# A cross-attention block: Fc's weight sums, some loads, and the last output projection placed and computed differently

## The chip, the cores and the metric

The kernel runs on one core of a Trainium2 chip. The metric is the device time of one execution in microseconds (us). Of three runs of the kernel before, the median is 766.39 us, the lowest 765.56 and the highest 767.55.

## The reference

One transformer block with cross-attention, in float32: batch 4, 512 positions, width 512, 16 heads of 32, MLP width 2048.

```python
residual = x
y = layer_norm(x, ln1_w, ln1_b)
q = (y @ q_w + q_b).reshape(B, LQ, H, HD).transpose(0, 2, 1, 3)
k = (enc @ k_w + k_b) ...        # enc: the other sequence, 512 positions too
v = (enc @ v_w + v_b) ...
scores = where(mask, q @ k^T / sqrt(HD), mask_value)
out = softmax(scores) @ v                      # back to B, LQ, D
hidden = out @ cproj_w + cproj_b + residual
y = layer_norm(hidden, ln2_w, ln2_b)
y = gelu_tanh(y @ fc_w + fc_b) @ proj_w + proj_b      # 512 -> 2048 -> 512
return hidden + y
```

## The kernel before

**Pairs.** The heads of a batch are taken in 4 groups of 4, so there are 16 windows w = 4 b + g, and each is done in two halves of 256 queries: 32 pairs p = 2 w + half (batch 0 is pairs 0 to 7, batch 3 pairs 24 to 31). `block` does one pair: TensorE writes 8 score tiles of 128x512 (`scores`, L317); VectorE adds the mask and takes the row minimum of the negated scores (L323); ScalarE takes the exponential with the row sums (L327); VectorE transposes the probabilities in squares of 32 into the tile tb (L335), of which there are two.

**The exchange.** The squares of tb have then to change places between groups of 32 partitions, into one tile of probabilities: pT, or for pairs 1, 3, 5, 7 the tile gt and for pairs 25, 27, 29, 31 the tile xe. `copies` does it: GpSimd copies the four squares that stay in their partitions (L393, 32x1088 each), and SyncE issues 12 DMAs for the others (L398). `attend` multiplies the result by v (L415, tile av), and VectorE scales it into oT (L420). There is one pT, so a pair's exchange is begun by `exchange` only when `attend` has read the pair before that in the same tile. From pair 10 on, `attend` of pair p - 2 runs at the start of pair p.

**The rest as filling.** The order on every engine is written out by hand: the program is recorded instruction by instruction and nothing reorders it. `put(p, ...)` lists what else is issued in pair p: projections of later windows (`prep_k` L255, `prep_q` L267, `prep_v`), layer norms, output projections, and, from pair 11 on by `some(n)`, the MLP of batches 0 and 1. Work of one item costs one product chain (3.4 in the planner's units, `CHAIN`) or two; `fill` deals it out between the steps of `block`.

**The MLP.** Fc works on pairs of 128-row chunks of fc_w by a form of Strassen's scheme: seven products of quarters in place of eight (`fc_seven`, products L576, sums on VectorE L530). Four sums of weight quarters are needed for each pair of chunks; GpSimd makes them ahead (`fc_sums`, four operations of 128x256 on wsum and pbt, L527 and L530), and for batch 0 stores them to DRAM by two DMAs of its own (L619, L620), as later batches read them again. `fc_sums` is called after every MLP item (in `fc_by_pair` and `proj`), directly behind `load_mlp`, and works on what has been loaded. wsum holds two sets. `proj` is the second MLP product (tile accp, L636).

**Layer norm of batches 1 and 3.** It is done on x transposed: `load_raw` loads the rows (tiles raw), the statistics come from a straight copy of x, `store_rn` and `load_rn` spread reciprocal deviation and mean over the partitions by way of DRAM (tiles rn), `ln1_rows` applies them on GpSimd (L218, 8 operations of 128x512) and `ln1_affine` weight and bias on ScalarE, into the tile xe, whose first half holds enc. Batches 0 and 2 use `load_x` and `ln1` (the items x1, x2, x3, and x4 = `load_enc`).

**Output projection.** `cproj(b, t)` multiplies 128 positions of oT by wc in four matmuls of 512 columns (L455, tile accc) and VectorE adds the result (L456) to h, which holds x and on which GpSimd has put the bias (`c_bias`, L426). Batch 3's h lies in the tile pbt.

**Queues.** Nearly all loads, the exchange, and batch 3's stores of h (tensor xa) are issued by SyncE, in one order; one of its DMAs is held until the eighth before it has landed. PSUM's eight banks are two pools of four, used in turns.

**The tail.** Behind pair 31 stand the last two `attend`, the MLP items left, `p_sums` (sums of proj's weight quarters, VectorE), batch 3's `cproj`, and `last_mlps`: the MLP of batches 2 and 3, whose weights for the next Fc pair are loaded by `load_wa`.

Of the kernel before, what the change touches and what calls it, by code (L numbers as in the profile page):

```python
# [12 lines left out]
F32 = mybir.dt.float32  # L13
# [38 lines left out]
def xattn_block(ctx: ExitStack, tc: tile.TileContext, x, rawT, encT, mask, q_w, k_w, v_w, c_w, fc_w, p_w, vecs, rows, out):  # L52
# [124 lines left out]
    def load_enc(b):  # L177
        for d in range(ND):
            queue(b).dma_start(out=eT[:, d, :], in_=encT[b, ts(d, P), :])
# [271 lines left out]
    def cproj(b, t):  # L451
# [5 lines left out]
        if not stays(b, t):  # L457
            (nc.sync if b == B - 1 else nc.gpsimd).dma_start(out=S["xa", b][ts(t, P), :], in_=h)

    def load_xn(b):  # L460

        for t in range(NT):
            S["h", b, t] = tiles.tile([P, D], F32, tag="xn", name=f"hn_{b}_{t}")
            Q[0].dma_start(out=S["h", b, t], in_=S["xa", b][ts(t, P), :])
# [144 lines left out]
    def fc_sums():  # L609

        while count[3] < len(fc_pairs) and count[3] < count[4] + 2:
            b, c = fc_pairs[count[3]]
            if ("fcw", b, 2 * c + 1) not in S:
                return
            x, y = raw_pair(b, c)
            s = wsum[:, count[3] % 2]
            a_sums(x[:, :2], x[:, 2:], y[:, :2], y[:, 2:], s[:, 0], s[:, 1], y[:, :2], s[:, 2], nc.gpsimd)
            if b == 0:
                nc.gpsimd.dma_start(out=sums_dram[c, :, :3], in_=s)  # L619
                nc.gpsimd.dma_start(out=sums_dram[c, :, 3], in_=y[:, :2])  # L620
            S["ws", b, c] = s[:, 0], s[:, 1], y[:, :2], s[:, 2]
            count[3] += 1

    def fc_by_pair(b, c):
        q, k = divmod(2 * c, FQ)
        fc_seven(b, c, gT[q % 2][:, k : k + 2, :], raw_pair(b, c), S["ws", b, c], acc_half, q % 2)
        count[1] += 2
        count[4] += 1
        load_mlp()
        fc_sums()  # L630

    def proj(b, q, t):
        gelus(q % 2)
        acc = acc_tile(f"accp_{b}_{q}_{t}")
        for k in range(FQ):
            nc.tensor.matmul(  # L636
                acc, gT[q % 2][:, k, ts(t, P)], S["pw", b, q * FQ + k], start=(k == 0), stop=(k == FQ - 1)
            )
        h = S["hid", b, t]
        nc.vector.tensor_tensor(h, acc, h, ALU.add)  # L640
        if q == NQ - 1:
            (nc.gpsimd if b == 0 else nc.sync).dma_start(out=out[b, ts(t, P), :], in_=h)
        count[1] += 1
        load_mlp()
        fc_sums()

# [22 lines left out]
    def last_mlps():  # L669
        last, = pools(ctx, last=1)  # L670
        ps_last = banks.pop()
        assert count[5] % 8 < 4
        count[5] = 0
        ga = last.tile([P, NP, 2, L], F32, tag="ga", name="ga")
        gs = last.tile([P, 3, NP, HL], F32, tag="gs", name="gs")
# [226 lines left out]
    def do(fn):  # L902
        return [(0.0, fn)]
# [62 lines left out]
    prep_v(0)  # L966
    prep_k(1)
    run(turns1(0))
    load_raw(1)
    load_h(0, *range(NT))  # L970
    nc.sync.dma_start(out=wc, in_=c_w)
    load_mlp()
# [24 lines left out]
    def h_(b, *ts_):  # L997
        return do(lambda: load_h(b, *ts_))
# [27 lines left out]
    k5, q5, v5 = A(5)  # L1026
    k6, q6, v6 = A(6)
    put(0, [(CHAIN, lambda: prep_v(1)), v2], do(lambda: store_rn(1)), [k2])
    put(1, [k3, (0.0, lambda: prep_q(1)), (CHAIN, lambda: (prep_v(3), load_enc(1), load_rn(1)))])
    put(2, [q2], [k4], do(lambda: ln1_rows(1, 0, 1)))  # L1030
    put(3, [q3, v4], do(lambda: ln1_rows(1, 2, 3)))
    put(4, [k5, v5], do(lambda: ln1_affine(1)))
    put(5, [q4, q5])
    put(6, [k6, q6])
# [10 lines left out]
    put(11, [k, v], some(2), pb_(0), mid=do(lambda: y_sums(0)))  # L1045

    x1, x2, x3, x4 = inputs(3)
    put(12, [q], some(2), x1)
    k, q, v = A(10)
    put(13, [k], some(2))  # L1050
    put(14, [q], some(2))
    put(15, x2[:1], V(10), x2[1:2], do(lambda: load_raw(3)), some(2), do(lambda: store_rn(3)), some(1),
        do(lambda: load_rn(3)), some(1))

    k, q, v = A(11)
    put(16, do(lambda: ln1_rows(3, *range(ND))), [k, q], some(2))
    put(17, h_(1, 0, 1), next_(lambda: ln1_affine(3)), h_(1, 2, 3), x4, cb(1), C(1))
    k, q, v = A(12)
    put(18, [q], some(2), [k])
    k, q, v = A(13)  # L1060
# [20 lines left out]
    for p in range(2 * NW):  # L1081
        w, half = divmod(p, 2)
        if half == 0 and w and w % NG == 0:
            make_mb(w // NG)
        run(ahead[p])
        for pair in due.get(p, ()):
            attend(*divmod(pair, 2))

        def fill(n, work=fills[p]):
            if n or not work or work[0][0] <= CHAIN:  # L1090
                run(work, CHAIN if n < 2 else None)

        block(w, half, fill, any(cost > CHAIN for cost, _ in fills[p]), mids[p])
# [3 lines left out]
    load_h(B - 1, *range(NT))  # L1097
    run(stat(2, 0, 1))
    attend(NW - 1, 0)
    run(some(2) + stat(2, 2, 3) + rs(2) + cb(B - 1) + norm(2, 0, 1) + some(2))  # L1100
    load_wa(first_c)
    attend(NW - 1, 1)
    run(mlp + norm(2, 2, 3))
    p_sums(first_c)
    load_wa(first_c + 1)
    c = C(B - 1)
    run(c[:2])
    p_sums(first_c + 2)
    run(c[2:])
    att.close()  # L1110
    last_mlps()

# [44 lines left out]
```

## Time and profile before

| | |
|---|---|
| median of three runs | 766.39 us (765.56 to 767.55) |
| profiled execution, its time | 765.46 us |
| its span, first to last instruction | 763.7 us |
| granted TensorE clock | 1.000 |
| busy: TensorE / VectorE / ScalarE / GpSimd | 757.0 / 591.2 / 336.5 / 329.3 us |
| chain that ended last | TensorE 93%, DMA 4%, SyncE's queue 2%, VectorE 1% |
| moved by DMA | 134.58 MB, mean 176 GB/s |

All times of the profile are of that one execution, on a clock that starts with its span; it took 0.93 us less than the median. PE is TensorE, DVE VectorE, ACT ScalarE, POOL GpSimd, SP SyncE, and SPq SyncE's queue of DMAs. In the timeline a row is a run of like instructions of one line, with its start, its length, and in brackets the idle time ahead of it with what ended it.

### The profile page before, as it was taken

The numbers are of one execution on the slowest core, as the hardware profiler recorded it, in microseconds if no ns is written. First come the engines' busy times: TensorE is split into PE (matmuls) and PEld (weight loads), VectorE is DVE, ScalarE is ACT, GpSimd is POOL, SyncE is SP. The second block draws the span as 40 slices with busy tenths as digits, with TensorE's granted clock in tenths as the row PEclk, the third lists the DMA queues.
The fourth block names the chain that finished last, engine by engine and source line by source line (L and its number), as shares of the span: only waits on it lengthen the run. The fifth ranks groups of instructions, "written<-read, shape, count | busy, mean of one in ns | idle before, by whom it ended". The sixth has DMA issues, their size and how long they took to land.

```text
span 763.7 us, 12836 instructions
## 1 busy us (share of the span) xinstructions
PE 757.0 (99%) x4346; PEld 512.8 (67%) x4346; DVE 591.2 (77%) x1186; ACT 336.5 (44%) x765; POOL 329.3 (43%) x347
## 2 busy tenths in 40 slices
PE   9999999999999999999999999999999999999998
PEld 7655455566574545475454566447888889988997
DVE  3888999879895777887887989855777886747862
ACT  2566766565773574637753567401202221022200
POOL 1538647368564874244575534430050014303152
PEclk9999999999999999999999999999999999999999
DMA  8999879467876686665756867783724402146001
GB/s 328 334 250 243 218 202 258 109 204 210 249 222 212 171 251 198 163 181 125 179 133 186 214 202 187 172 291 131 268 98 135 163 27 90 35 135 217 1 15 42
DMA packets 60576, 134.58 MB, mean 176 GB/s; under 512 B 11312, under 2 KB 17072, under 8 KB 60384
## 3 DMA queue, kind: packets, MB, share of 16 engines
q1 hardware_dynamic: 58448, 126.73, 57.3%
q0 software_dynamic: 1920, 7.01, 2.8%
q8 instruction: 35, 0.57, 0.3%
q14 instruction: 29, 0.24, 0.1%
q10 hardware_dynamic: 144, 0.02, 0.0%
HBM read 69.23 MB, written 11.02 MB: 105 GB/s over the span
## 4 chain that ended last, share of the span: by engine, by line
PE 93%; DMA 4%; SPq 2%; DVE 1%; issue 0%; POOL 0%; POOLq 0%
PE q L576 24%; PE accp L636 11%; PE r L723 8%; PE av L415 8%; PE accc L455 7%; PE sc L317 7%; PE acck L255 7%; PE accq L267 6%; PE accv L278 3%; PE accv L298 3%; PE q4p L759 2%; PE q1p L777 2%; SPq L398 2%; PE tp L166 1%; DMA pbt<-fc_w_dram 1%; DMA ptt<-v_w_dram 1%
## 5 line engine op out<-in xcount | busy, mean ns | idle before, releaser
L327 ACT ACTIVATE ptt<-ptt,mn 128x512 f32<-128x512 f32 x256 | 181.6, 711 | 143.0 <-DVE mn L323 142.9
L323 DVE CUSTOM_DVE_ANT_0 ptt<-sc,mb 128x512 f32<-128x512 f32 x256 | 160.6, 682 | 19.3 <-PE sc L317 19.2
L335 DVE STREAM_TRANSPOSE tb<-ptt 128x1024 f32<-128x1024 f32 x128 | 153.3, 1217 | 0.0
L393 POOL COPY pT<-tb 32x1088 f32<-32x1088 f32 x96 | 104.7, 1090 | 58.8 <-DMA pbt<-p_w_dram 19.0
L636 PE MATMUL accp<-pbt,gt 128*128 128x512 f32 x192 | 84.8, 595 | 0.0
L576 PE MATMUL q<-yT,gt 128*128 128x256 f32 x320 | 78.9, 379 | 0.0
L597 ACT ACTIVATE ga<-ga,vec 128x512 f32<-128x512 f32 x40 | 26.7, 714 | 92.3 <-DVE ga L530 92.3
L576 PEld LDWEIGHTS q<-yT,gt 128*128 128x128 f32 x320 | 60.8, 190 | 8.7 <-issue 0.2
L636 PEld LDWEIGHTS accp<-pbt,gt 128*128 128x128 f32 x192 | 35.9, 190 | 45.1 <-issue 39.9
L317 PE MATMUL sc<-pbt 32*128 32x512 f32 x512 | 65.3, 614 | 0.0
L576 PE MATMUL q<-ys,gt 128*128 128x256 f32 x240 | 61.6, 379 | 0.0
L255 PE MATMUL acck<-xe,ptt 128*128 128x512 f32 x128 | 58.5, 600 | 0.7 <-DVE tb L335 0.7
L267 PE MATMUL accq<-xe,ptt 128*128 128x512 f32 (+1 forms) x136 | 58.5, 574 | 0.0
L455 PE MATMUL accc<-wc,oT 128*128 128x512 f32 x128 | 56.5, 597 | 0.0
L530 DVE TENSOR_TENSOR ga<-q,ga 128x512 f32<-128x512 f32 (+1 forms) x60 | 36.2, 603 | 21.8 <-PE q L576 20.0
L576 PEld LDWEIGHTS q<-ys,gt 128*128 128x128 f32 x240 | 45.6, 190 | 6.2
L327 ACT ACTIVATION_READ_ACCUMULATOR ptt<-ptt,mn 128x1 f32 x256 | 47.8, 187 | 0.0
L415 PE MATMUL av<-pT,v 128*32 128x256 f32 x768 | 46.4, 382 | 1.4 <-DMA pT<-tb 0.7
L267 PEld LDWEIGHTS accq<-xe,ptt 128*128 128x128 f32 x136 | 24.9, 190 | 31.4 <-issue 22.5
L455 PEld LDWEIGHTS accc<-wc,oT 128*128 128x128 f32 x128 | 23.8, 190 | 31.6 <-issue 27.2
L255 PEld LDWEIGHTS acck<-xe,ptt 128*128 128x128 f32 x128 | 23.4, 191 | 31.6 <-issue 22.2
L317 PEld LDWEIGHTS sc<-pbt 32*128 32x128 f32 x512 | 27.3, 183 | 24.9 <-issue 15.8
(190 smaller groups left out, 1228.4 us busy)
## 6 DMA issues: line engine op xcount, KB each, us to landing
pT<-tb SPq DMA_DIRECT2D x288, 136.0 KB, 2.4
pbt<-p_w_dram SPq DMA_DIRECT2D x40, 256.0 KB, 3.8
gt<-ws SPq DMA_DIRECT2D x20, 512.0 KB, 3.4
gt<-tb SPq DMA_DIRECT2D x48, 136.0 KB, 4.3
xe<-tb SPq DMA_DIRECT2D x48, 136.0 KB, 2.8
pbt<-fc_w_dram SPq DMA_DIRECT2D x24, 256.0 KB, 3.5
gt<-fc_w_dram SPq DMA_DIRECT2D x20, 256.0 KB, 3.3
ptt<-k_w_dram SPq DMA_DIRECT2D x16, 256.0 KB, 3.3
```

Of the source, the lines that this page charges most:

```text
L255: nc.tensor.matmul(acc, S["wk", w][:, d, :], eT[:, d, :], start=(d == 0), stop=(d == ND - 1))
L267: nc.tensor.matmul(acc, S["wq", w][:, d, :], xT[:, d, c], start=(d == 0), stop=(d == ND - 1))
L317: nc.tensor.matmul(S["sc", w, qt][h], qT[r, ts(qt, P)], kT[r, :], start=True, stop=True)
L323: nc.vector.tensor_tensor_reduce(out=s, in0=S["sc", w, qt][h], in1=S["mb", w // NG], scale=1.0, scalar=FMAX, op0=ALU.add, op1=ALU.min, acc ...
L327: nc.scalar.activation(s, s, AF.Exp, bias=mn, scale=-1.0, accum_out=S["sums", w][:, qt, h : h + 1])
L335: nc.vector.transpose(tv[:, qt % 2, 2 * k : 2 * k + 2], S["ps", w, qt, k])
L393: nc.gpsimd.tensor_copy(pT[ts(i, HD), i], tb[ts(i, HD), i])
L415: nc.tensor.matmul(av[ts(h, HD), : 2 * P].rearrange(shape, **kw), v[:, t, ts(h, HD)], p[t][h], start=(t == 0), stop=(t == NT - 1),)
L455: nc.tensor.matmul(acc, S["oT", b][:, g, ts(t, P)], wc[:, g, :], start=(g == 0), stop=(g == NG - 1))
L576: nc.tensor.matmul(o, x[:, k], y[:, k], start=(k == 0), stop=(k == 1))
L636: nc.tensor.matmul(acc, gT[q % 2][:, k, ts(t, P)], S["pw", b, q * FQ + k], start=(k == 0), stop=(k == FQ - 1))
L723: nc.tensor.matmul(r, x[:, c], w[:, c], start=(c == 0), stop=(c == NP // 2 - 1))
```

## The change

1. Batch 3's output projection is no longer four `cproj` but `cproj_last`: the 512x512x512 product is cut into quarters and done by seven products of 256 (q1 to q7), each with four matmuls of 256 columns. The sums of wc's quarters go into the tile wct, those of oT's into oTt (both take the place of a tb); the results are joined with h on VectorE, three of the joins on GpSimd. The parts stand between the remaining MLP items, and the layer norm of positions 256 to 511 of batch 2 (`norm(2, 2, 3)`) goes behind them.
2. `fc_sums` is no longer called behind each MLP item but once a pair, after `attend`, for p > 10, and by that behind the exchange's copies.
3. Batch 1's raw rows (`load_raw(1)`) are loaded in pair 1 instead of at the start, its spread rows (`load_rn(1)`) in pair 2 instead of 1, and `ln1_rows` of batch 1 stands as a whole in pair 3.
4. x of batch 3 (x1) is loaded in pair 14 instead of 12; the first two tiles of h of batch 1 in pair 16 instead of 17.

```diff
+    def cproj_last():
+        b = B - 1
+        wt, ot = (two.tile([P, NI, PW + 2 * HD], F32, tag="tb", name=n) for n in ("wct", "oTt"))
...
+        a11, a21, a12, a22 = (S["oT", b][:, 2 * k : 2 * k + 2, ts(i, HL)] for k in range(2) for i in range(2))
+        w11, w12, w21, w22 = (wc[:, 2 * k : 2 * k + 2, ts(j, HL)] for k in range(2) for j in range(2))
+        t1, t2, t4, p1, u2, u3 = (wt[:, n] for n in range(6))
+        s1, s2, s4 = (ot[:, n] for n in range(3))
+        s3, t3 = a21, w12
...
+        def product(n, x, w):
+            q[n] = acc_half(f"q{n}c")
+            for t in range(2):
+                for k in range(2):
+                    nc.tensor.matmul(q[n][:, t], x[:, k, ts(t, P)], w[:, k], start=(k == 0), stop=(k == 1))
+        def join(engine, i, j, src):
+            o = h[:, 2 * i : 2 * i + 2, ts(j, HL)]
+            add(engine, o, src, o)
...
+        def one():
+            b_sums(w11, w12, w21, w22, t1, t2, t3, t4)
+            sub(s3, a11, a21)
+        def two_():
+            product(1, a11, w11)
+            nc.scalar.copy(p1, q[1])
+            product(2, a12, w21)
+        def three():
+            product(7, s3, t3)
+        def sums():
+            sub(s2, a22, s3)
+            sub(s4, a12, s2)
+            add(nc.vector, s1, s2, a11)
+        def four():
+            product(6, s2, t2)
+            add(nc.vector, u2, q[6], p1)
+            product(3, s4, w22)
+            add(nc.vector, u3, q[7], u2)
+            product(5, s1, t1)
+            join(nc.gpsimd, 1, 0, u3)
+            join(nc.gpsimd, 1, 1, u3)
+            join(nc.gpsimd, 0, 1, u2)
+            join(nc.vector, 0, 0, q[1])
+            join(nc.vector, 0, 0, q[2])
+        def five_():
+            product(4, a22, t4)
+            join(nc.vector, 0, 1, q[3])
+            join(nc.vector, 0, 1, q[5])
+            for t in range(2):
+                store(t)
+            join(nc.vector, 1, 1, q[5])
+            join(nc.vector, 1, 0, q[4])
+            for t in range(2, 4):
+                store(t)
...
     def fc_by_pair(b, c):     # and the same line in proj
         load_mlp()
-        fc_sums()
...
-    load_raw(1)
...
-    put(1, [k3, (0.0, lambda: prep_q(1)), (CHAIN, lambda: (prep_v(3), load_enc(1), load_rn(1)))])
-    put(2, [q2], [k4], do(lambda: ln1_rows(1, 0, 1)))
-    put(3, [q3, v4], do(lambda: ln1_rows(1, 2, 3)))
+    put(1, [k3, (0.0, lambda: prep_q(1)), (CHAIN, lambda: (prep_v(3), load_enc(1), load_raw(1)))])
+    put(2, [q2], [k4], next_(lambda: load_rn(1)))
+    put(3, [q3, v4], do(lambda: ln1_rows(1, *range(ND))))
...
-    put(12, [q], some(2), x1)
+    put(12, [q], some(2))
-    put(14, [q], some(2))
+    put(14, [q], some(2), x1)
...
-    put(16, do(lambda: ln1_rows(3, *range(ND))), [k, q], some(2))
-    put(17, h_(1, 0, 1), next_(lambda: ln1_affine(3)), h_(1, 2, 3), x4, cb(1), C(1))
+    put(16, do(lambda: ln1_rows(3, *range(ND))), [k, q], some(2), h_(1, 0, 1))
+    put(17, next_(lambda: ln1_affine(3)), h_(1, 2, 3), x4, cb(1), C(1))
...
             attend(*divmod(pair, 2))
+        if p > 10:
+            fc_sums()
...
     attend(NW - 1, 0)
-    run(some(2) + stat(2, 2, 3) + rs(2) + cb(B - 1) + norm(2, 0, 1) + some(2))
+    c = cproj_last()
+    c[0]()
+    run(some(2) + do(c[1]) + stat(2, 2, 3) + rs(2) + cb(B - 1) + norm(2, 0, 1) + some(1) + do(c[2]))
     load_wa(first_c)
     attend(NW - 1, 1)
-    run(mlp + norm(2, 2, 3))
+    c[3]()
+    run(mlp)
+    c[4]()
     p_sums(first_c)
     load_wa(first_c + 1)
-    c = C(B - 1)
-    run(c[:2])
+    c[5]()
+    run(norm(2, 2, 3))
     p_sums(first_c + 2)
-    run(c[2:])
```

**TensorE, the tail.** Before, from the av of pair 30 to the first Fc of batch 2 (accp are MLP projections of batch 1, accc the output projection of batch 3; L455, L636):

```order
L415 MATMUL av_0_4395<-pT_0_4246,v_3508 32x256 x16
L636 MATMUL accp_1_0_4413<-pbt,gt 128x512 x4
L636 MATMUL accp_1_1_4419<-pbt,gt 128x512 x4
L636 MATMUL accp_1_2_4441<-pbt,gt 128x512 x4
L636 MATMUL accp_1_3_4447<-pbt,gt 128x512 x4
L415 MATMUL av_1_4460<-xe,v_3508 32x256 x16
L455 MATMUL accc_0_4487<-wc,oT_3710 128x512 x4
L455 MATMUL accc_1_4494<-wc,oT_3710 128x512 x4
L455 MATMUL accc_2_4505<-wc,oT_3710 128x512 x4
L455 MATMUL accc_3_4512<-wc,oT_3710 128x512 x4
L576 MATMUL q_1_4_4533<-yT_3367,gt 128x256 x2
```

The same place of the change, where the seven products are q1c to q7c and Fc's line is now L646, that of the MLP projections L705:

```order
L705 MATMUL accp_1_1_4426<-pbt,gt 128x512 x4
L479 MATMUL q1c<-wc,oT_3710 128x256 x4
L479 MATMUL q2c<-wc,oT_3710 128x256 x4
L705 MATMUL accp_1_2_4459<-pbt,gt 128x512 x4
L479 MATMUL q7c<-wc,oT_3710 128x256 x4
L415 MATMUL av_1_4473<-xe,v_3508 32x256 x16
L705 MATMUL accp_1_3_4494<-pbt,gt 128x512 x4
L479 MATMUL q6c<-wct,oTt 128x256 x4
L479 MATMUL q3c<-wc,oTt 128x256 x4
L479 MATMUL q5c<-wct,oTt 128x256 x4
L479 MATMUL q4c<-wct,oT_3710 128x256 x4
L646 MATMUL q_1_4_4566<-yT_3367,gt 128x256 x2
```

Three products now stand ahead of the last av, one MLP projection behind it, and four products between that and Fc.

**SyncE, the start.** Before, from the last v weight to pair 1's exchange; the raw loads stand further up, behind the first weights:

```order
L248 DMA ptt<-v_w_dram 128x512
L179 DMA xe<-encT_dram 128x512 x4
L213 DMA rn_0_499<-rn_381 128x512
L213 DMA rn_1_500<-rn_381 128x512
L398 DMA gt<-tb_1_410 32x1088 x12
L248 DMA ptt<-q_w_dram 128x512
```

The same place of the change (rn and raw are the tiles of batch 1, rn_373 the DRAM tensor that is spread):

```order
L248 DMA ptt<-v_w_dram 128x512
L179 DMA xe<-encT_dram 128x512 x4
L200 DMA raw_0_491<-rawT_dram 128x512
L200 DMA raw_1_492<-rawT_dram 128x512
L200 DMA raw_2_493<-rawT_dram 128x512
L200 DMA raw_3_494<-rawT_dram 128x512
L398 DMA gt<-tb_1_402 32x1088 x12
L248 DMA ptt<-q_w_dram 128x512
L248 DMA ptt<-k_w_dram 128x512
L213 DMA rn_0_580<-rn_373 128x512
L213 DMA rn_1_581<-rn_373 128x512
```

Four raw loads are now between enc (tile xe) and the exchange into gt, and the two rn loads are behind it.

**GpSimd, pair 11.** Before, ahead of the copies into pT (h is that of batch 0, the wsum rows are `fc_sums`):

```order
L309 TENSOR_TENSOR v_1724<-v_1724,row 128x512
L530 TENSOR_TENSOR wsum<-pbt 128x256
L527 TENSOR_TENSOR pbt<-pbt 128x256
L527 TENSOR_TENSOR wsum<-wsum,pbt 128x256
L527 TENSOR_TENSOR wsum<-pbt,wsum 128x256
L619 DMA ws<-wsum 128x768
L620 DMA ws<-pbt 128x256
L426 TENSOR_TENSOR h_0_234<-h_0_234,row 128x512
L426 TENSOR_TENSOR h_1_236<-h_1_236,row 128x512
L426 TENSOR_TENSOR h_2_238<-h_2_238,row 128x512
L426 TENSOR_TENSOR h_3_240<-h_3_240,row 128x512
L393 COPY pT_1_1799<-tb_1_1663 32x1088 x4
```

The same place of the change, with `fc_sums` at L597 and L600:

```order
L309 TENSOR_TENSOR v_1724<-v_1724,row 128x512
L426 TENSOR_TENSOR h_0_226<-h_0_226,row 128x512
L426 TENSOR_TENSOR h_1_228<-h_1_228,row 128x512
L426 TENSOR_TENSOR h_2_230<-h_2_230,row 128x512
L426 TENSOR_TENSOR h_3_232<-h_3_232,row 128x512
L393 COPY pT_1_1793<-tb_1_1663 32x1088 x4
L600 TENSOR_TENSOR wsum<-pbt 128x256
L597 TENSOR_TENSOR pbt<-pbt 128x256
L597 TENSOR_TENSOR wsum<-wsum,pbt 128x256
L597 TENSOR_TENSOR wsum<-pbt,wsum 128x256
L689 DMA ws<-wsum 128x768
L690 DMA ws<-pbt 128x256
```

The six instructions of `fc_sums` have gone from ahead of the bias and the copies to behind them.

More of the change, by code (lines that the diff above doesn't have):

```diff
@@ L458, in cproj, with store @@
             (nc.sync if b == B - 1 else nc.gpsimd).dma_start(out=S["xa", b][ts(t, P), :], in_=h)
+    def cproj_last():
+        b = B - 1
+        wt, ot = (two.tile([P, NI, PW + 2 * HD], F32, tag="tb", name=n) for n in ("wct", "oTt"))
+        wt, ot = (
+            x.rearrange("p i n -> p (i n)")[:, : 8 * D].rearrange("p (n i f) -> p n i f", n=8, i=2) for x in (wt, ot)
+        )
+        a11, a21, a12, a22 = (S["oT", b][:, 2 * k : 2 * k + 2, ts(i, HL)] for k in range(2) for i in range(2))
[3 more added lines that the diff above has]
+        s3, t3 = a21, w12
+        h = pbt[:, : NT * D].rearrange("p (t n) -> p t n", t=NT)
+        q = {}
+        def product(n, x, w):
[6 more added lines that the diff above has]
+            add(engine, o, src, o)
+        def store(t):
+            nc.sync.dma_start(out=S["xa", b][ts(t, P), :], in_=S["h", b, t])
+        def one():
[32 more added lines that the diff above has]
+                store(t)
+        return one, two_, three, sums, four, five_
@@ L644, in proj @@
         load_mlp()
-        fc_sums()
     wa = [gt[:, i * 2048 : i * 2048 + 1024].rearrange("p (i d f) -> p i d f", i=2, d=ND) for i in range(2)]
@@ L671, in last_mlps @@
         ps_last = banks.pop()
-        assert count[5] % 8 < 4
         count[5] = 0
```

## Prediction

> **What bounds the kernel now.** I read the page first, then TensorE's timeline end to end, and only where it pauses the other engines' timelines.
>
> ```profile
> PE 757.0 (99%) x4346; PEld 512.8 (67%) x4346; DVE 591.2 (77%) x1186; ACT 336.5 (44%) x765; POOL 329.3 (43%) x347
> ```
>
> TensorE is busy in 757.0 of 763.7 us, so the time is its stream of products plus its pauses, and a change can only shorten the stream, remove a pause, or make one. The timeline's start times show pauses better than busy time does, as matmuls overlap. First a regular stretch and the three irregular ones behind it (columns: start, length, engine, line, operation, tiles; in brackets the idle time and who ended it):
>
> ```profile
> 171.15 1.89 PE L576 MATMUL q<-yT,pbt 128*128 128x256 f32 x8
> 177.29 1.93 PE L415 MATMUL av<-pT,v 128*32 128x256 f32 x32
> ...
> 184.62 1.89 PE L576 MATMUL q<-yT,pbt 128*128 128x256 f32 x8
> ...
> 191.24 1.93 PE L415 MATMUL av<-pT,v 128*32 128x256 f32 x32 [0.41 <-POOL pT L393]
> 193.10 2.00 PE L317 MATMUL sc<-pbt 32*128 32x512 f32 x16
> 195.03 3.70 PE L255 MATMUL acck<-xe,ptt 128*128 128x512 f32 x8
> 198.57 1.89 PE L576 MATMUL q<-yT,pbt 128*128 128x256 f32 x8
> ...
> 205.09 1.93 PE L415 MATMUL av<-pT,v 128*32 128x256 f32 x32 [0.32 <-DVE gt L530]
> ...
> 219.30 1.93 PE L415 MATMUL av<-pT,v 128*32 128x256 f32 x32 [0.67 <-DMA pT<-tb]
> ```
>
> An Fc pair takes 177.29 - 171.15 = 6.14 us from its start to the next product; at 184.62 it takes 6.62, a pause of 0.48. A whole pair of that stretch without a pause is 1.86 (av) + 1.93 (scores) + 3.54 (k) + 6.14 = 13.47 us; the next two take 13.85 and 14.21, pauses of 0.38 and 0.74. Two more places pause, at batch 1's first k and at the scores of pair 18:
>
> ```profile
> 48.49 3.70 PE L267 MATMUL accq<-xe,ptt 128*128 128x512 f32 x8
> 52.93 3.67 PE L255 MATMUL acck<-xe,ptt 128*128 128x512 f32 x8 [0.73 <-DVE tb L335]
> ```
>
> ```profile
> 280.42 2.54 PE L317 MATMUL sc<-pbt 32*128 32x512 f32 x16
> ```
>
> Eight products of 512 columns are 3.54 us (195.03 to 198.57), so 52.93 is 0.9 late; scores take 2.54 instead of 2.00 at 280.42, a pause of 0.54 within them. These five pauses make 3.04 us; that and the stream itself are all there is to win.
>
> **Part 1, the seven products.** The old output projection of batch 3, and one 256-column product of another stage:
>
> ```profile
> 507.55 14.00 PE L455 MATMUL accc<-wc,oT 128*128 128x512 f32 x32
> 521.39 1.89 PE L576 MATMUL q<-yT,gt 128*128 128x256 f32 x8
> ...
> 549.01 3.62 PE L759 MATMUL q2p<-pbt,ga 128*128 128x256 f32 x16
> 552.47 2.13 PE L166 MATMUL tp<-ident,h 128*128 128x128 f32 x16
> ```
>
> The 32 rows (16 matmuls, two rows each) take 13.84 us. Sixteen rows of 256 columns take 552.47 - 549.01 = 3.46, so the narrow form costs half of the wide one. A new product has 4 matmuls, 8 rows, 1.73 us; seven cost 12.11. **Term: -1.73 us.**
>
> In the order of TensorE given with the change, the last MLP projection (accp_1_3, 3.5 us) now stands between the last av and q6, and covers the three DVE sums of oT that q6, q3 and q5 need (about 0.7 each, 2.1 with the product of r before them 2.5). The sums of wc run an MLP projection earlier. What may be late is DVE behind q6. Fc restarts at 521.39 - 1.73 = 519.66, so q6 ends four products before the last, at 514.5, and u3 is added by 516.2. After it DVE has 2 joins, 4 sums of proj's weights, 4 joins, 2 normalisations and 4 sums: 16 operations of 0.68 or less (row of 552.19 below), 10.5 us, so 526.7. TensorE goes on without it until the third Fc pair reuses a bank, at 519.66 + 2 x 6.04 + 0.86 = 532.6; less one add of 0.69, DVE may be at 531.9. Slack 5.2 us, term nothing; the price if it is gone is in the last rival. SP's four stores of xa wait for these joins, with the next weight loads queued behind them; those are needed at 531.7.
>
> **Part 2, batch 1's raw rows.** SP's queue, and the landing of enc (46 to 53 us) and of pair 1's exchange (50 to 61 us):
>
> ```profile
> 47.37 1.88 SPq L179 DMA_DIRECT2D xe<-encT_dram  x4
> 49.29 0.98 SPq L213 DMA_DIRECT2D rn<-rn  x2
> 50.47 9.86 SPq L398 DMA_DIRECT2D gt<-tb  x12
> ```
>
> ```profile
> DMA to landing us min/median/max: 5.9/6.0/6.1
> ```
>
> ```profile
> DMA to landing us min/median/max: 5.2/5.3/5.5
> ```
>
> ```profile
> ptt<-k_w_dram SPq DMA_DIRECT2D x16, 256.0 KB, 3.3
> 67.53 1.93 PE L415 MATMUL av<-gt,v 128*32 128x256 f32 x32
> ```
>
> acck at 52.93 is the first product that reads batch 1's enc: issued at 47.37, it lands 5.9 later, at 53.3 at most. So it is the transfer, though the row names DVE. It cannot be issued earlier (the last v of batch 0 reads that tile), but what is ahead of it can go: without four raw loads at the start, SP does pair 0's exchange and three weights earlier, and these are landed by then. Between 5.9 and the 3.3 of a lone weight, enc lands at 50.7 to 53.3; wanted is 52.0.
>
> In SP's order the four raw loads stand where the two rn loads stood, and these go behind the exchange. They take about 1.9, as enc's four do, instead of 0.98, so the exchange starts 0.9 later. Before, its last DMA was issued at 60.33 and landed 5.3 later, at 65.6; its av came at 67.53, a margin of 1.9. With TensorE 0.9 earlier 0.1 is left, so some of the gain may come back here. Bounds: -0.92 to +0.7 (nothing gained, and the exchange's own length up by 1.7, as four loads ahead of it do at 193.75 below: 0.9 + 1.7 - 1.9); I take **-0.75**, as the late weights are gone from the queue by then. GpSimd's eight row operations of batch 1 now stand in one piece ahead of the copies of pair 3:
>
> ```profile
> 70.46 5.21 POOL L218 TENSOR_TENSOR raw<-raw,rn 128x512 f32<-128x512 f32 x4
> ```
>
> ```profile
> 89.42 1.93 PE L415 MATMUL av<-gt,v 128*32 128x256 f32 x32
> ```
>
> Four more make 5.2, so the copies (4.5, row of 186.71 below) end at 70.46 + 5.21 + 5.2 + 4.5 = 85.4, before their av: nothing.
>
> **Part 3, Fc's sums behind the copies.** GpSimd, on the same clock, one answer per stretch:
>
> ```profile
> 177.35 0.72 POOL L530 TENSOR_TENSOR wsum<-pbt 128x256 f32<-128x256 f32 x1
> ...
> 181.79 4.97 POOL L426 TENSOR_TENSOR h<-h,row 128x512 f32<-128x512 f32 x4
> 186.71 4.48 POOL L393 COPY pT<-tb 32x1088 f32<-32x1088 f32 x4
> ```
>
> The sums and their two stores (177.35 to 181.79, 4.4 us) have moved from ahead of the bias and the copies to behind them, so the copies end at 186.8 instead of 191.2, and the pause at 191.24 goes whole: **-0.48**. The two later pauses end with the exchange's DMAs, not with copies. SP:
>
> ```profile
> 191.28 1.81 SPq L184 DMA_DIRECT2D xn<-x_dram  x4
> 193.75 9.15 SPq L398 DMA_DIRECT2D pT<-tb  x12
> ...
> 207.59 8.65 SPq L398 DMA_DIRECT2D pT<-tb  x12
> ...
> 246.43 7.49 SPq L398 DMA_DIRECT2D pT<-tb  x12
> ```
>
> Twelve DMAs take 7.49 us alone. At 193.75 they take 9.15 behind four loads of x (now two pairs later), at 207.59 8.65, with the sums' stores beside them (now behind). Given back are 1.66 and 1.16 us, where 0.38 and 0.74 were lost; but new stores of half a megabyte now follow the exchange closely. Bounds: both pauses gone, or both kept; I take **-0.3** and **-0.6**, most of it, by the row of 246.43. The loads of x now stand in pair 14 and the statistics that read them in pair 15, 8 us later, more than the 5.9 to 6.1 that four such loads took to land above: nothing. That sums come later costs nothing if they are there for Fc. The tightest is the last:
>
> ```profile
> 458.68 8.34 SPq L398 DMA_DIRECT2D xe<-tb  x12
> ```
>
> ```profile
> 467.55 1.03 PE L576 MATMUL q<-ys,wsum 128*128 128x256 f32 x4
> ```
>
> Copies can start with the exchange, 458.7, and end at 463.2; three sums of 0.8 are done by 465.6, and Fc reads the third at 467.55: 1.9 us to spare.
>
> **Part 4, h of batch 1 loaded earlier, at pair 16.**
>
> ```profile
> 276.32 0.69 DVE L456 TENSOR_TENSOR h<-accc,h 128x512 f32<-128x512 f32 x1 [5.22 <-POOL h L426]
> ```
>
> ```profile
> 275.03 3.72 POOL L426 TENSOR_TENSOR h<-h,row 128x512 f32<-128x512 f32 x3 [2.45 <-DMA h<-x_dram]
> ```
>
> DVE waits 5.22 for the bias on h, and that for the load. Two of the four loads now go ahead of the exchange of pair 16 (12 DMAs, 8 us), so the first bias waits only for copies and sums, about 272.5: DVE gets 2.5 us back, and the 0.54 at the scores goes. Bounds 0 and -0.54; I take **-0.5**.
>
> **Sum.** -1.73 - 0.75 - 0.48 - 0.3 - 0.6 - 0.5 = -4.36. The profiled execution took 765.46 (span 763.7), so 761.1 on its own scale; the median of the runs, 766.39, is 0.93 above it, so **762.0**.
>
> **Two rules against the change.** The sums' stores are issued by GpSimd, the exchange by SP. The Trainium skill, "DMA: Bandwidth & Descriptors", section "Issuing engines are not separate DMA queues", says that all of them run on the same 16 DMA engines and interleave. The stretch at 207.59 agrees (8.65 with the stores, 7.49 without), and by this rule stores that follow closely could still hold up the last landings: the first rival. The other rule bears on DVE behind q6:
>
> ```profile
> 552.19 0.68 DVE L527 TENSOR_TENSOR pbt<-pbt 128x512 f32<-128x512 f32 x1
> 552.79 1.77 DVE L527 TENSOR_TENSOR ptt<-pbt,ptt 128x512 f32<-128x512 f32 x1
> ```
>
> ```profile
> 552.73 6.31 POOL L426 TENSOR_TENSOR hl<-hl,row 128x512 f32<-128x512 f32 x4 [44.17 <-DVE ptt L527]
> ```
>
> Beside GpSimd's adds a DVE sum takes about 1.77 instead of 0.68. The Trainium skill, "SBUF — State Buffer", section "SBUF: two separate sides", calls this an exclusive lock: a DVE operation with two SBUF inputs and one of GpSimd never run together. The rows agree in direction. Here GpSimd joins three blocks (up to 1.58 each, 4.7 us) while DVE sums proj's weights, which by these rows puts about three DVE operations at 1.1 more, 3.3 of the 5.2 us of slack.
>
> **Rivals.** (1) The exchange sets the pace whatever stands around it: the pauses at 205 and 219 stay, since av, its DVE product, twelve DMAs and a landing form a loop of 14 us with one pT; for it, both pauses ended with DMAs. The gain is 4.36 - 0.9 = 3.5, and 762.9. (2) Only the products pay, as a pause that goes comes back at the next place (the exchange of pair 1, late sums, a landing): 766.39 - 1.73 = 764.7. For it is the 0.1 us left at pair 1. (3) Slower: DVE behind q6. If the port keeps it slow beyond the three joins, with 1.1 us more for each of its sixteen operations, TensorE waits at the third Fc pair as soon as five are slowed; nine undo the whole gain; all sixteen cost 17.4 - 5.2 = 12.2, so 774.2. Against it: GpSimd has no other work there. That the change does not move what it says is excluded by the orders above.
>
> **Numbers.** Forecast 0.55, (1) 0.20, (2) 0.15, (3) 0.10, since the slack of part 1 is the least certain number here. About 0.3%, 2.3 us, is what a measurement tells from no change: the forecast and (1) are faster by more (0.75), (2) is within it, (3) slower. The low end takes every term at its bound (-1.73, -0.92, -0.48, -0.38, -0.74, -0.54, in all -4.79, 761.6) and 0.8 for the spread of the runs (765.56 to 767.55): 760.8. The high end takes (2) in, with 0.5 of that spread: 765.2.
>
> **What would show it.** Right: seven products of 1.73 between the last av and Fc; no bracket at the av of pairs 11 to 13 and at batch 1's first k; scores of pair 18 in 2.00; a twelve-DMA exchange near 7.5 there. Wrong: DVE more than 5 us behind TensorE at the third Fc pair after the products; a bracket at the av of pair 1; an Fc product that waits for GpSimd's wsum; the pauses at 205 and 219 unchanged.

## The result, and the profile after

The changed kernel takes 763.59 us (median of nine runs, 762.21 to 765.70), the kernel before beside it 766.26 (764.78 to 767.55). The ratio is 0.9968, 95% interval 0.9956 to 0.9981: 2.5 us less (the interval is 1.5 to 3.4). The forecast was 762.0, the range 760.8 to 765.2.

The page after, first row of busy times, then TensorE's timeline at the places of the prediction (span 761.7 us):

```profile
PE 757.0 (99%) x4370; PEld 517.8 (68%) x4370; DVE 600.9 (79%) x1198; ACT 337.1 (44%) x766; POOL 334.3 (44%) x350
```

```profile
52.54 3.60 PE L255 MATMUL acck<-xe,ptt 128*128 128x512 f32 x8
...
68.93 3.39 PE L317 MATMUL sc<-pbt 32*128 32x512 f32 x16
72.25 3.70 PE L255 MATMUL acck<-xe,ptt 128*128 128x512 f32 x8
...
81.31 2.55 PE L317 MATMUL sc<-pbt 32*128 32x512 f32 x16
```

```profile
192.19 1.93 PE L415 MATMUL av<-pT,v 128*32 128x256 f32 x32
205.66 1.93 PE L415 MATMUL av<-pT,v 128*32 128x256 f32 x32
219.12 1.93 PE L415 MATMUL av<-pT,v 128*32 128x256 f32 x32
```

```profile
280.25 2.00 PE L317 MATMUL sc<-pbt 32*128 32x512 f32 x16
```

```profile
508.63 3.70 PE L705 MATMUL accp<-pbt,gt 128*128 128x512 f32 x8
512.16 1.89 PE L479 MATMUL q6c<-wct,oTt 128*128 128x256 f32 x8
...
519.07 1.89 PE L646 MATMUL q<-yT,gt 128*128 128x256 f32 x8
...
543.24 3.92 PE L844 MATMUL q1p<-pbt,ga 128*128 128x256 f32 x16
547.00 3.62 PE L826 MATMUL q2p<-pbt,ga 128*128 128x256 f32 x16
```

Every pause that the prediction named is gone: no bracket at 52.54, 13.47 us between the av rows twice, 2.00 us for the scores at 280.25. Three places are new. The scores of pairs 4 and 5 take 3.39 and 2.55 us instead of 2.00, and q1p, the first proj product of batch 2, takes 3.76 from its start to the next instead of 3.45. The rows of the trace before, for pair 4 and q1p:

```profile
69.39 2.00 PE L317 MATMUL sc<-pbt 32*128 32x512 f32 x16
...
545.56 3.62 PE L777 MATMUL q1p<-pbt,ga 128*128 128x256 f32 x16
```

Aligned piece by piece with the trace before, TensorE's stream moves like this (us; minus is earlier):

| place | forecast | measured |
|---|---|---|
| start of the run, up to the scores at 47.08 | none | +0.51 |
| batch 1's first k | -0.75 | -0.90 |
| scores of pair 4 | none | +1.39 |
| scores of pair 5 | none | +0.48 |
| av of pairs 11, 12, 13 | -0.48, -0.3, -0.6 | -0.48, -0.38, -0.75 |
| scores of pair 18 | -0.5 | -0.47 |
| the seven products | -1.73 | -1.65 |
| q1p | none | +0.31 |

The named terms make -4.63, the three new pauses +2.18, together -2.45, close to the ratio's 2.5 us. The first row lies between -0.4 and +0.6 in the traces below, as against the trace before, and is put down to no edit; with it the two spans differ by 2.0.

VectorE shows what the two pauses at the scores wait for: at pair 3 and pair 4 the transposes into tb stand still. The row of pair 3 before, which has no bracket, then the two rows after:

```profile
63.23 2.37 DVE L335 STREAM_TRANSPOSE tb<-ptt 128x1024 f32<-128x1024 f32 x2
```

```profile
64.59 2.37 DVE L335 STREAM_TRANSPOSE tb<-ptt 128x1024 f32<-128x1024 f32 x2 [1.74 <-DMA gt<-tb]
...
76.13 2.37 DVE L335 STREAM_TRANSPOSE tb<-ptt 128x1024 f32<-128x1024 f32 x2 [1.32 <-ACT ptt L327]
```

The transpose that writes a tb first has to wait until the exchange of two pairs earlier has read it, as there are two tb. SyncE's queue shows how late that exchange is:

```profile
47.56 1.85 SPq L179 DMA_DIRECT2D xe<-encT_dram  x4
49.45 2.15 SPq L200 DMA_DIRECT2D raw<-rawT_dram  x4
51.72 9.41 SPq L398 DMA_DIRECT2D gt<-tb  x12
```

Pair 1's exchange now starts at 51.72 instead of 50.47, and the transposes of pair 3 begin at 64.59 instead of 63.23, although TensorE is 0.46 us earlier there. VectorE being late, the score tiles come free late, and TensorE waits at the next scores. The theory that the experiments test: the raw loads, moved ahead of pair 1's exchange, cost more by the tile tb than they gain at the first k. The rivals: the two pauses are an accident of this execution; or the row operations in one piece make them.

### The profile page after: what moved, and what is told of

It is laid out like the page before. It is cut to its first block, busy times and chain, and to the rows that moved or that the text cites. A ratio compares the mean times of both kernels' runs of the same rounds, so it can differ in the third digit from the quotient of the medians.

```text
span 761.7 us, 12895 instructions
## 1 busy us (share of the span) xinstructions
PE 757.0 (99%) x4370; PEld 517.8 (68%) x4370; DVE 600.9 (79%) x1198; ACT 337.1 (44%) x766; POOL 334.3 (44%) x350
## 4 chain that ended last, share of the span: by engine, by line
PE 99%; POOL 0%; DVE 0%; issue 0%; POOLq 0%
PE q L646 25%; PE accp L705 11%; PE sc L317 8%; PE r L790 8%; PE av L415 8%; PE acck L255 7%; PE accq L267 7%; PE accc L455 6%; PE accv L278 5%; PE accv L298 3%; PE q1p L844 2%; PE q4p L826 2%; PE tp L166 1%; PE warm L1023 1%; PE q3p L826 0%; PE q5p L826 0%
## 5 line engine op out<-in xcount | busy, mean ns | idle before, releaser
L705 PE MATMUL accp<-pbt,gt 128*128 128x512 f32 x192 | 85.3, 596 | 0.0
L646 PE MATMUL q<-yT,gt 128*128 128x256 f32 x320 | 78.9, 379 | 0.0
L646 PEld LDWEIGHTS q<-yT,gt 128*128 128x128 f32 x320 | 60.8, 190 | 8.3
L705 PEld LDWEIGHTS accp<-pbt,gt 128*128 128x128 f32 x192 | 35.8, 190 | 44.7 <-issue 39.1
L646 PE MATMUL q<-ys,gt 128*128 128x256 f32 x240 | 61.6, 379 | 0.0
L600 DVE TENSOR_TENSOR ga<-q,ga 128x512 f32<-128x512 f32 (+1 forms) x60 | 36.2, 603 | 17.4 <-PE q L646 15.0
L646 PEld LDWEIGHTS q<-ys,gt 128*128 128x128 f32 x240 | 45.6, 190 | 6.2
L455 PE MATMUL accc<-wc,oT 128*128 128x512 f32 x96 | 42.5, 598 | 0.0
L309 POOL TENSOR_TENSOR v<-v,row 128x512 f32<-128x512 f32 x16 | 20.3, 1277 | 46.4 <-ACT v L283 37.3
```

The costliest lines, as they stand in the source:

```text
L455: nc.tensor.matmul(acc, S["oT", b][:, g, ts(t, P)], wc[:, g, :], start=(g == 0), stop=(g == NG - 1))
L646: nc.tensor.matmul(o, x[:, k], y[:, k], start=(k == 0), stop=(k == 1))
L705: nc.tensor.matmul(acc, gT[q % 2][:, k, ts(t, P)], S["pw", b, q * FQ + k], start=(k == 0), stop=(k == FQ - 1))
```

## The experiments

**The raw rows at the start again** (part 3 of the change undone, the rest kept):

```diff
     run(turns1(0))
+    load_raw(1)
     load_h(0, *range(NT))
...
-    put(1, [..., (CHAIN, lambda: (prep_v(3), load_enc(1), load_raw(1)))])
-    put(2, [q2], [k4], next_(lambda: load_rn(1)))
-    put(3, [q3, v4], do(lambda: ln1_rows(1, *range(ND))))
+    put(1, [..., (CHAIN, lambda: (prep_v(3), load_enc(1), load_rn(1)))])
+    put(2, [q2], [k4], do(lambda: ln1_rows(1, 0, 1)))
+    put(3, [q3, v4], do(lambda: ln1_rows(1, 2, 3)))
```

> The changed kernel with part 3 of the change undone: batch 1's raw rows are loaded at the start again, its spread rows in pair 1, and its row operations stand in two pieces. Theory (the raw loads hold up pair 1's exchange, whose DMAs read the tile tb that VectorE's transposes of pair 3 write next; pauses of 1.39 and 0.50 us at the scores of pairs 4 and 5, against 0.97 won at batch 1's first k): the pause at the first k is back at about 0.9 us, the scores of pairs 4 and 5 take 2.00 us, VectorE does not wait for DMAs of gt, and the kernel takes about 0.9 us less than the changed one, 762.7 against 763.6. Rival (the two pauses come from the other three parts or from this run alone): they stay, and the kernel takes 0.9 us more than the changed one, 764.5.

762.36 us (761.92 to 762.61; ratio to before 0.9953, 0.9939 to 0.9968), 1.2 less than the changed kernel by the medians, though the intervals of the two ratios overlap. TensorE and VectorE at the place:

```profile
52.25 3.67 PE L255 MATMUL acck<-xe,ptt 128*128 128x512 f32 x8
...
68.71 2.88 PE L317 MATMUL sc<-pbt 32*128 32x512 f32 x16
71.52 3.70 PE L255 MATMUL acck<-xe,ptt 128*128 128x512 f32 x8
```

```profile
63.86 2.37 DVE L335 STREAM_TRANSPOSE tb<-ptt 128x1024 f32<-128x1024 f32 x2 [1.23 <-ACT ptt L327]
```

The time came as expected, the pauses only in part: 0.28 at the first k and 0.88 at the scores of pair 4, together 1.16 against 1.87 with the raw rows ahead of the exchange; pair 5 has none. So the order of the kernel before has the wait at tb as well. The row names ScalarE, but this transpose needs the second exponential of the pair only, done at 61.0. What is left of its waits are the exchange's DMAs, and the trace's semaphore updates, which none of the rows shown prints, settle it: pair 1's, issued up to 60.04, had all landed at 63.58, and the transposes begin at 63.86. In the changed kernel the last landing is at 64.46 and they begin at 64.59; in the profile before it is at 62.69, and VectorE had other work until 63.23.

**The raw rows ahead of enc**, in a gap of SyncE's queue:

```diff
-    put(1, [k3, (0.0, lambda: prep_q(1)), (CHAIN, lambda: (prep_v(3), load_enc(1), load_raw(1)))])
+    put(1, [k3, (0.0, lambda: (prep_q(1), load_raw(1))), (CHAIN, lambda: (prep_v(3), load_enc(1)))])
```

> The changed kernel with one move: the four raw loads are issued ahead of batch 1's enc, right behind the projection of q in pair 1, where SyncE's queue stood idle from 44.2 to 47.2 us; nothing new stands between enc and pair 1's exchange. Theory (the place of the raw loads ahead of the exchange is the cause): the exchange starts at about 49.5 us instead of 51.7, VectorE's transposes of pair 3 wait for no DMA, both pauses of 1.39 and 0.50 go; if enc, now behind a megabyte, still lands in 5 us, the first k has no pause and the kernel takes 1.9 us less than the changed one, 761.7; if it lands later, up to 0.9 is lost again, 762.6. Rival (not the place of the loads but the row operations in one piece delay pairs 4 and 5): the pauses stay at about 1.9 together, 763.6.

762.67 us (761.97 to 764.11; ratio 0.9958, 0.9942 to 0.9974). The exchange of pair 1 starts at 49.67, the transposes of pair 3 at 63.69 with no wait, and the scores of pairs 4 and 5 take 2.00.

```profile
49.67 9.30 SPq L398 DMA_DIRECT2D gt<-tb  x12
```

But enc lands late:

```profile
52.55 3.09 PE L255 MATMUL acck<-xe,ptt 128*128 128x512 f32 x6 [0.77 <-DMA xe<-encT_dram]
55.94 1.12 PE L255 MATMUL acck<-xe,ptt 128*128 128x512 f32 x2 [0.30 <-DMA xe<-encT_dram]
57.00 1.93 PE L415 MATMUL av<-pT,v 128*32 128x256 f32 x32
```

The pause of 0.9 is back and another of 0.85 stands within the four products of k. The place of the raw loads decides what is late, as the theory has it, and the row operations, still in one piece here, make no pause. The megabyte ahead of enc cost 0.85 more than the 0.9 that was allowed for it: in all 1.75 against the changed kernel's 1.87. That the median is 0.9 lower, at the 762.6 of the expectation's second case, these pauses don't explain: they differ by 0.1, and the intervals of the ratios overlap.

**The products alone** (the kernel before with part 1):

> The kernel before with part 1 of the change alone, the seven products of batch 3's output projection with the order of the tail. Theory (7 products for 32 rows of 512 columns, and VectorE's backlog behind q6 reaches the last gelu of the next Fc, where TensorE waits 0.3 us): stretch from the last av to the first Fc product, with the three products ahead of it, 1.65 to 1.73 us shorter; the first proj product of batch 2 takes 3.76 us instead of 3.45; in all 1.3 to 1.4 us less than before, about 764.9. Rival (VectorE's backlog does not reach TensorE; the 0.3 us was of that run alone): 1.7 us less, 764.5.

764.79 us (764.05 to 766.28; ratio 0.9979, 0.9967 to 0.9991), 1.7 less than before by the medians. The trace has -1.66 at the products (+1.73 at the last av, -3.39 at Fc) and +0.30 at q1p:

```profile
544.51 3.92 PE L846 MATMUL q1p<-pbt,ga 128*128 128x256 f32 x16
```

So the 0.3 belongs to the products, and is no accident of one run. Time alone could not tell the two theories apart.

**The sums alone** (the kernel before with part 2; x of batch 3 still in pair 12):

> The kernel before with part 2 of the change alone: Fc's weight sums behind the exchange's copies, x of batch 3 still loaded in pair 12. Theory (the stores of the sums and the copies behind them made the pauses ahead of the av of pairs 11, 12 and 13): all three pauses of 0.48, 0.38 and 0.74 us go, 1.6 us less than before, 764.7. Rival (the middle pause comes from the loads of x ahead of that exchange, so that it needs their move): 0.48 goes, 0.38 stays, and of the 0.74 what the late stage before it leaves; 0.5 to 1.2 us less.

770.21 us (769.61 to 771.65; ratio 1.0059, 1.0044 to 1.0074): slower than before by 3.7 by the medians and 4.5 by the ratio, which neither side expected.

```profile
190.08 1.93 PE L415 MATMUL av<-pT,v 128*32 128x256 f32 x32
...
207.44 3.64 PE L415 MATMUL av<-pT,v 128*32 128x256 f32 x32 [3.82 <-DMA pT<-tb]
211.01 3.16 PE L317 MATMUL sc<-pbt 32*128 32x512 f32 x16
```

```profile
190.60 2.40 SPq L184 DMA_DIRECT2D xn<-x_dram  x4
193.09 10.56 SPq L398 DMA_DIRECT2D pT<-tb  x12
```

The first of the two stores before, then both in this run:

```profile
194.60 0.56 POOL L619 DMA_DIRECT2D ws<-wsum  x1 [0.30 <-POOL wsum L527]
```

```profile
200.54 0.56 POOL L619 DMA_DIRECT2D ws<-wsum  x1 [0.30 <-POOL wsum L527]
201.10 0.54 POOL L620 DMA_DIRECT2D ws<-pbt  x1
```

The pause ahead of pair 11's av is gone, as expected. But four loads of x stand ahead of pair 12's exchange, which takes 10.56 us, and GpSimd's stores of the sums, now behind the copies, are issued at 200.5 in its second half; before they came at 194.6, at its start. The pause ahead of the av is 3.9 us in place of 0.38, so that it comes 3.5 later. 2.9 more is lost behind that, by the clock that TensorE is granted. PEclk has that clock in tenths of full speed, in 40 slices of the span, with 9 for 90% or more, and this run's page has the one lowered digit of all the pages:

```profile
PEclk9999999999899999999999999999999999999999
```

TensorE stands idle from 203.62 to 207.44; from 206.58 to 213.41 the trace grants it a clock of 0.50, and there the av takes 3.57 instead of 1.86 and the scores 3.09 instead of 1.93. The mean clock of the four runs of this kernel is 0.996 to 0.998, that of the kernel before beside them 0.999 to 1.000.

**x of batch 3 alone**, in pair 14 (the kernel before):

```diff
-    put(12, [q], some(2), x1)
+    put(12, [q], some(2))
...
-    put(14, [q], some(2))
+    put(14, [q], some(2), x1)
```

> The kernel before with one step of part 3's neighbours alone: x of batch 3 loaded in pair 14 instead of 12; Fc's sums stay ahead of the copies. Theory (the loads of x lengthen the exchange at 193.75 and so make the pauses ahead of the av of pairs 12 and 13; the sums make only the one ahead of pair 11): 0.48 us stays at 191, 0.38 and 0.74 go, 1.1 us less than before, 765.4. Rival (the sums ahead of the copies hold GpSimd's copies, and with them the av, at all three places): all three stay, 766.5; in this case neither step alone pays, and only both together gain the 1.6 us seen in the changed kernel.

766.11 us (764.49 to 767.98; ratio 0.9996, 0.9981 to 1.0010): no gain that can be told.

```profile
192.16 1.93 PE L415 MATMUL av<-pT,v 128*32 128x256 f32 x32 [0.40 <-POOL pT L393]
205.63 1.93 PE L415 MATMUL av<-pT,v 128*32 128x256 f32 x32
219.99 1.93 PE L415 MATMUL av<-pT,v 128*32 128x256 f32 x32 [0.82 <-DVE gt L530]
```

The pause ahead of pair 12's av (0.38) goes, those of 11 and 13 stay; with the sums alone it was these two that went. Neither theory holds as put: x makes the middle pause, the sums the two others, and the 1.6 us seen in the changed kernel's trace need both edits.

**The stores held back to the next pair's copies** (the sums alone, as above, and this; `store_late` issues the two stores of the pair before, behind the first of the four copies):

```diff
+            if i == 0:
+                store_late()
...
-                nc.gpsimd.dma_start(out=sums_dram[c, :, :3], in_=s)
-                nc.gpsimd.dma_start(out=sums_dram[c, :, 3], in_=y[:, :2])
+                late.append((sums_dram[c, :, :3], s))
+                late.append((sums_dram[c, :, 3], y[:, :2]))
```

> The kernel before with Fc's sums behind the copies and x of batch 3 still in pair 12 (which took 770.2), and one further move: the two stores of each set of sums are held back to the next pair, where they stand behind the first of the four copies, at the start of the exchange instead of in its second half. Theory (stores of half a megabyte, issued while the last DMAs of an exchange lengthened by the loads of x are still to land, hold up those landings): the av of pair 12 no longer waits 3.5 us, and the pauses of 1.7 and 1.2 behind it go; 765 to 766. Rival (the four loads of x just ahead of the exchange do it alone): the pauses of 3.5, 1.7 and 1.2 stay, 770.

766.25 us (763.58 to 769.57; ratio 1.0007, 0.9992 to 1.0021), 4 less than with the stores in the second half.

```profile
190.73 2.49 SPq L184 DMA_DIRECT2D xn<-x_dram  x4
193.31 8.90 SPq L405 DMA_DIRECT2D pT<-tb  x12
```

```profile
204.45 1.93 PE L422 MATMUL av<-pT,v 128*32 128x256 f32 x32 [0.71 <-DMA pT<-tb]
217.92 1.93 PE L422 MATMUL av<-pT,v 128*32 128x256 f32 x32
```

With the same loads of x ahead of it, the exchange takes 8.90 and its av waits 0.7 instead of 3.8, and the clock stays at 1.000. So the stores in the second half make the large pause, once the loads of x have lengthened the exchange. The runs of this kernel spread over 6 us and the profiled one is the shortest. The two longest have a mean clock of 0.998, so that the lowered clock may be back in them; what they wait for is open.

**The changed kernel again**, unedited:

> The changed kernel once more, without an edit, on the chip of the two runs beside it. Theory (the pauses of 1.39 and 0.50 us at the scores of pairs 4 and 5 belong to the change): about 1.9 us together in this execution too, with VectorE's transposes of pair 3 waiting for the exchange of pair 1. Rival (an accident of the first execution): gone, and a span 1.9 us shorter.

763.67 us (761.76 to 767.10; ratio 0.9968, 0.9952 to 0.9983), span 761.8.

```profile
64.26 2.37 DVE L335 STREAM_TRANSPOSE tb<-ptt 128x1024 f32<-128x1024 f32 x2 [2.01 <-DMA gt<-tb]
...
76.02 2.37 DVE L335 STREAM_TRANSPOSE tb<-ptt 128x1024 f32<-128x1024 f32 x2 [1.53 <-DMA pT<-tb]
```

Pauses of 1.67 and 0.69 at pairs 4 and 5: no accident of the first execution. The second wait too is now put down to the exchange of two pairs before, where the first trace named ScalarE; by the semaphore updates that exchange had landed at 76.01 in the first trace and at 75.90 here, 0.1 ahead of the transposes in both.

**The sums of proj's weights ahead of the last av** (the changed kernel):

```diff
     load_wa(first_c)
+    p_sums(first_c)
     attend(NW - 1, 1)
...
     c[4]()
-    p_sums(first_c)
```

> The changed kernel with one move: the four sums of proj's weights that VectorE makes behind q6 (first pair of chunks) are made ahead of the last av, where VectorE was idle for 2.9 us. Theory (VectorE's backlog behind q6 is handed on through the next four Fc pairs to the last gelu, where TensorE waits 0.31 us): four operations, of which two took 1.64 and 1.75 us beside GpSimd's joins, leave the backlog; the first proj product of batch 2 takes 3.45 us instead of 3.76, and the kernel 0.3 us less. Rival (the joins themselves, or ScalarE's order, make the wait): 3.76 stays.

```profile
542.67 3.62 PE L844 MATMUL q1p<-pbt,ga 128*128 128x256 f32 x16
546.13 3.62 PE L826 MATMUL q2p<-pbt,ga 128*128 128x256 f32 x16
```

q1p takes 3.46 again, so the 0.3 was VectorE's backlog. The time, 764.84 (762.45 to 766.73; ratio 0.9974, 0.9957 to 0.9992), doesn't show so little. At the scores of pair 4 this trace loses 1.72, like the changed kernel, and at those of pair 5 nothing: with this order the first pause is in all three traces, the second in two.

**Fc's first weights late, the raw rows at the start:**

```diff
     nc.sync.dma_start(out=wc, in_=c_w)
-    load_mlp()
...
-    put(9, c[:1], do(lambda: attend(3, 1)), ...
+    put(9, do(load_mlp), c[:1], do(lambda: attend(3, 1)), ...
```

> The changed kernel with the raw rows loaded at the start again (as in the kernel before), and in their place the eight first loads of Fc's weights (2 MB, not read before pair 10) moved from the start to pair 9. Theory (SyncE's queue and the DMA engines are full in the first 60 us: enc of batch 1 then lands 5.6 to 6.1 us after its issue, and the exchange of pair 1 so late that the transposes of pair 3 wait for its tile): enc lands in about 3.6 us as in the changed kernel, no pause at the first k, no wait of the transposes, 1.2 us less than with the raw rows at the start alone: 761.2. Rival (the loads ahead of the exchange, here the two spread rows, decide, not the load at the start): pauses of 0.3 and 0.9 us as with the raw rows at the start, 762.4; or the 2 MB in pair 9 hold up the exchange there, and a new pause appears at the av of pairs 9 to 11.

761.45 us (761.12 to 763.42; ratio 0.9935, 0.9916 to 0.9954).

```profile
52.33 3.60 PE L255 MATMUL acck<-xe,ptt 128*128 128x512 f32 x8
...
68.71 2.00 PE L317 MATMUL sc<-pbt 32*128 32x512 f32 x16
70.64 3.70 PE L255 MATMUL acck<-xe,ptt 128*128 128x512 f32 x8
```

The first k has no pause and the scores of pair 4 take 1.93: both are won at once. Enc lands 4.5 to 4.7 us after its issue, not 3.6 as expected, which is enough. The time is 2.1 less than the changed kernel's by the medians, and the intervals of the two ratios don't meet. A pause of 1.8 ahead of pair 13's av stands in this trace, whose execution is the longest of the six; the expectation of the next run puts it at 1.1.

**Both moves together:**

> Both moves that the earlier runs speak for, on top of the changed kernel: raw rows at the start again with Fc's first weights loaded in pair 9 in their place, and the sums of proj's weights made ahead of the last av. Theory (the two pauses are independent of each other): no pause at batch 1's first k, at the scores of pairs 4 and 5 and at the first proj product of batch 2; 1.9 + 0.3 us less than the changed kernel's profile, about 761.2 by the clock of its median, and 5 us less than the kernel before. Rival (the 1.1 us pause ahead of the av of pair 13, seen with Fc's weights in pair 9, belongs to that move): it is there again, and the kernel takes about 762.3.

762.54 us (761.61 to 763.65; ratio 0.9952, 0.9939 to 0.9964). Its profiled execution has a span of 759.8, the shortest of the profiled ones, with none of the three new pauses and none at pair 13, so that one does not always come with the move.

```profile
69.03 2.00 PE L317 MATMUL sc<-pbt 32*128 32x512 f32 x16
...
541.44 3.62 PE L844 MATMUL q1p<-pbt,ga 128*128 128x256 f32 x16
```

The median is 1.3 above the expectation and 1.1 above that of the first move alone, so the second move shows in the trace and not in the time; it is also near the rival's 762.3, and what the executions without a trace wait for is open. Both kernels beat the one before; against the changed kernel (763.67 beside this one) both medians are lower, though the intervals of this one's ratio and the changed kernel's overlap.

## Why the prediction was right, and where a step failed

The time lies in the range, by terms that came nearly as worked out and one that was wrong. It is 1.6 us above the forecast, and the range holds it because its high end took rival (2) in, not because this loss was foreseen. Parts are numbered here as in the list of the change; the prediction has the raw rows as its part 2 and the sums as its part 3.

- **Products:** -1.65 for -1.73; one product is 1.73 us (512.16 to 519.07 is four in 6.91).
- **VectorE behind q6:** the backlog ends at 527.45, forecast 526.7, with two operations slowed beside GpSimd's joins (1.64 and 1.75), not three. The third Fc pair starts at 531.16 without a wait, so the last rival did not come. But "term nothing" was 0.31 short: the lateness is handed on from Fc to Fc and is seen where a gelu is read at once, at q1p. Making four sums earlier removed it.
- **Sums, x and h:** -0.48, -0.38, -0.75, -0.47 for -0.48, -0.3, -0.6, -0.5. The first rival is excluded: both pauses went, with twelve DMAs in 7.5 and 7.7 us. Its mechanism is real nevertheless: the stores cost 3.5 us at one av where loads of x still lengthened the exchange, and the lowered clock 2.9 more. The prediction took the move of x for part of a small gain; without it part 2 loses 3.7 us.
- **Raw rows:** the failed step. The forecast -0.75 at the first k came as -0.90, but the cost of a later exchange was looked for at its av only ("a margin of 1.9"). What else waits for it was left out: the transposes that write the same tb two pairs on, in the profile before 4.3 us ahead of that av. The margin was misread too. The 5.3 us is from a view that has the landing of only two of the twelve DMAs, issued at 54.20 and 54.87; by the semaphore updates the last landed at 62.69, not 65.6. So the av had 4.8 us to spare and the transposes, at 63.23, 0.5. With the same order but for other parts of the change that landing came at 63.58 and 63.63 and they had to wait (the raw rows at the start, the products alone). In net part 3 costs 0.97 in the first trace (-0.90 + 1.39 + 0.48); undoing it saves 1.2 us by the medians, within what the intervals leave open.
- **The profile before was one of the lucky ones.** Six executions ran the old order there. The wait at pair 4 is nothing or 0.12 in three (the profile before, the sums alone, the stores held back), and 0.75 to 1.27 in three (the products alone, the raw rows at the start, x alone). An operation that escapes a wait by little has no bracket to tell of it.
- **The second rival**, that a pause which goes comes back at the next place, held for part 3 alone, at pair 1's exchange as it named, but by tb and not by the av.

## What to carry to other kernels

A transfer that is made later has two ends: who reads what it writes, and who overwrites what it reads; with two buffers the second may come first. When an order is edited for a queue, test each edit alone and with its companion: here one lost 3.7 us alone, its companion gained nothing alone, and together they gained 1.6 in the trace. Where a wait for several semaphores names an engine that has long been done, look at the DMAs that hold the same tile.

## What the runs showed of the hardware

The landing of one and the same load of enc, issued from 47 us on, hangs on what was queued up to 30 us ahead of it: 5.0 to 6.4 us in the six traces with raw rows and Fc's first weights both loaded at the start, 3.5 to 4.7 in the three without the raw rows there, 3.8 to 4.7 in the two without Fc's weights (with that edit alone 5.6 to 5.8 became 4.5 to 4.7).

Each DMA of the exchange updates its semaphore 16 times, and the last update can be far behind the others: at pair 1's last DMA the sixteenth comes 1.5 us after the fifteenth in the changed kernel, 1.9 with x alone, 1.3 with the products alone, and 0.5 in the profile before. What holds it back is open.

TensorE's clock fell to half 3.0 us into the idle stretch of 3.8 us in the trace of the sums alone, and was full again 6.0 us after the products went on. Idle stretches of up to 1.8 us within the stream (pair 13 with Fc's weights late) did not lower it; the other traces have it lowered only behind the last product.

The Trainium skill, "DMA: Bandwidth & Descriptors", section "Issuing engines are not separate DMA queues", says that DMAs issued by different engines share the same 16 DMA engines and interleave; the kernel with the sums alone agrees, where two stores issued by GpSimd in the second half of an exchange issued by SyncE held its av up by 3.5 us more than before, and the same two issued at its start (the stores held back) by 0.4 more.
